# Summing a graph layer's spare blocks by node on VectorE in place of one-hot products on TensorE

## The chip, the cores and the metric

The kernel runs on one core of one Trainium2 chip. The metric is the device time of one execution in microseconds; the time of a kernel is the median of several runs.

## The reference

A graph of 6250 nodes with 256 channels and 100,000 edges (`src`, `dst`, with `dst` sorted) goes through four layers. In each, every node adds to its own row the rows of the sources of its edges, and a small network with three weight matrices follows:

```python
def agg(h):
    return jax.ops.segment_sum(h[src], dst, num_segments=N)
for l in range(NL - 1):                      # layers 0, 1, 2
    h = x + agg(x)
    h = jax.nn.relu(h @ W1s[l] + b1s[l])
    h = jax.nn.relu(h @ W2s[l] + b2s[l])
    x = h @ W3s[l] + b3s[l]
h = x + agg(x)                               # layer 3, the head
h = jax.nn.relu(h @ cW1 + cb1)
h = jax.nn.relu(h @ cW2 + cb2)               # 64 channels
return h @ cW3 + cb3
```

Before the first layer `x` is layer-normalized and rectified; at the end the given `x` is added. All of it is fp32. Since a layer is linear up to its first bias, the kernel keeps rows already multiplied by the next layer's W1, so that a layer starts with the sum over edges and then adds the bias.

## The kernel before

The nodes are cut into 49 blocks of 128. `sorted_edges` sums a block's edges in one of two ways.

- **Multiplied blocks.** The edge counts between all source nodes and the block's 128 nodes form a matrix, which layer 0 builds once (`build`, L1002) from one-hot products: 32 bf16 products `bp` a block (L1024), their one-hots `lo` and `hi` made on VectorE (L983), the sums cast to uint8 by ScalarE or VectorE (L1032, L1034), and the block written to a DRAM matrix (`mats`). Up to four blocks are a panel. `product` (L1450) runs over a panel in 49 units, one for each block of source nodes. A unit is four matmuls `agg` (L1469): the two halves of the 256 channels, and for each the high and the low part of the rows (`XY` holds both for all 49 blocks). The panel's counts are fetched by SyncE (`fetch`, L1043) and cast to fp32 into a ring `a` by ScalarE (L1444) or VectorE (L1446) some units ahead.
- **Gathered blocks.** `Gathered` (L1248) fetches the rows of the edges by indirect DMA on GpSimd, 128 edges a time and 18 times a block (L1293), and adds them up on TensorE with one-hots of 32 columns (`sums`, L1337), which VectorE makes (L1318), in two visits a block. VectorE then adds the block's own row and the sums into `u` (L1354, L1363), TensorE turns it (`pt`, L1371), and ScalarE adds bias and rectifies (L1379).

Both kinds then go through `mlp` (L1128): second product (L1140, or L1154 in the head), third product (L1203, L1184), and the result is stored to the next layer's table in DRAM and split again into high and low part in `XY` (`split`, `reload`).

Layer 0 has 27 multiplied blocks in seven panels and 22 gathered ones; layers 1 to 3 have 31 multiplied blocks in eight panels, the first of three blocks, and 18 gathered ones.

The order is written out by hand: every engine's instructions come in the order in which the program issues them. `product` advances unit by unit; a planner keeps a clock of its own in which every step has a price (`passed`, `work_of`), and spreads the gathers of a layer evenly over its expected length (`Gathered.begin`, `flow`, `send`), each tied by `after` to a TensorE instruction. A layer's gathers begin when the last store of the layer before has been issued. `LEAD` (21 us) is how far rows are asked for ahead of their visit.

Ahead of layer 0 comes the setup: `look` (L604) finds for each half block where its edges begin (`first`), asks for the edges by indirect DMA on GpSimd (`ask`, L598; eight requests are issued at once behind `starts`), and turns them into the one-hot codes `clT` and the gather lists `idx` and `rel`; `normed` (L811) normalizes, multiplies by W1 and stores the first table, interleaved step by step with `look`. If `look` finds the edges unfit (`good` is 0), the general program `any_edges` runs behind.

Of the kernel before, what the change touches and what calls it, by code (L numbers as in the profile page):

```python
# [8 lines left out]
F32 = mybir.dt.float32  # L9
I32 = mybir.dt.int32  # L10
# [386 lines left out]
def sorted_edges(  # L397
# [72 lines left out]
    S0 = 2 * panels[0][0]  # L470
    assert gone[-2] == panels[-1] and sorted(
        b + i for b, n in gone[:-2] + gone[-1:] + panels for i in range(n)) == list(range(NT))
# [13 lines left out]
    clT = const.tile([P, 2, GSUB, NSUB - S0], BF16, name="clT")  # L486
# [7 lines left out]
    tables = [dram.tile([N, C], F32, name=f"table{l}") for l in range(NLAYER + 1)]  # L494
    w31d = [dram.tile([P, (KC + 1) * C], F32, name=f"w31_{l}") for l in range(NLAYER)]
    mats = [dram.tile([P, n, NT * P], U8, name=f"mat{p}") for p, (_, n) in enumerate(panels)]
# [107 lines left out]
    def look(pool):  # L604
# [27 lines left out]
        junk = pool.tile([P, NEAR], BF16, name="junk", bufs=1)  # L632
        for h in range(2):
# [5 lines left out]
                                    op0=OP.is_lt, op1=OP.add, accum_out=half[:NSUB, h:h + 1])  # L639
        at = pool.tile([P, 1], F32, name="at_f", bufs=1)  # L640
# [15 lines left out]
        place = pool.tile([P, 1], F32, name="place", bufs=1)  # L656
        nc.gpsimd.iota(place, pattern=[[0, 1]], base=0, channel_multiplier=P,
# [43 lines left out]
        for q in range(NQ):  # L701
            nc.tensor.matmul(ps[:PW, 2 * q:2 * q + 2], sel[:NSUB, q, :], both[:NSUB, :],
                             start=True, stop=True)
        spread = pool.tile([P, NQ, 2], F32, name="spread", bufs=1)
# [7 lines left out]
        for q, (b, _) in enumerate(gone):  # L712
            nc.vector.tensor_scalar(part[:PW, q:q + 1], part[:PW, q:q + 1], place[:PW, 0:1],
                                    float(T * P * b), op0=OP.add, op1=OP.add)
# [16 lines left out]
        for q0 in range(0, GSUB, H):  # L731
# [180 lines left out]
    with tc.manual_schedule():  # L912
# [38 lines left out]
        def load_weights(l):  # L951
# [15 lines left out]
        batches = [(p, s, q0) for p, (b0, n) in enumerate(panels)  # L967
                   for s in range(2 * b0, 2 * (b0 + n)) for q0 in range(0, GSUB, BATCH)]
# [4 lines left out]
        def pair(hots, k):  # L973

            if k < len(batches):
                s = batches[k][1]
                pairs[s] = hots.tile([P, 2, GSUB, 2], BF16, name="pairs", bufs=3)
                nc.scalar.copy(pairs[s], clT[:, :, :, s - S0, None].to_broadcast([P, 2, GSUB, 2]))
# [23 lines left out]
        def build(hots, ats, ps_b):  # L1002
# [7 lines left out]
            for k, (p, s, q0) in enumerate(batches):  # L1010
                i, half = divmod(s - 2 * panels[p][0], 2)
# [5 lines left out]
                for q in range(0, BATCH, 2):  # L1017
# [17 lines left out]
                    if half and q0 + q + 2 == GSUB:  # L1035
                        own = at[:, panels[p][0] + i, :]
                        nc.vector.tensor_tensor(own, own, ident, OP.add)
                        nc.sync.dma_start(out=mats[p][:, i, :], in_=at.rearrange("p h d -> p (h d)"))
# [4 lines left out]
        def fetch(l, p):  # L1043

            n = panels[p][1]
            c = len(mat.setdefault((l, p), [])) * P
            at = chunks.tile([P, 4, CH * P], U8, name="at", bufs=5)
            nc.sync.dma_start(out=at[:, :n, :], in_=mats[p][:, :, c:c + CH * P])
# [199 lines left out]
        class Gathered:  # L1248
            def __init__(self, l):
# [3 lines left out]
                               for q, (b, n) in enumerate(gone) for i in range(n)  # L1253
                               if l == 0 or (b, n) != panels[-1]]
                self.alone = {b + i for b, n, i, _ in self.blocks}
                self.visits = [(g, rounds) for g in range(len(self.blocks)) for rounds in VISITS[l > 0]]
# [136 lines left out]

        EARLY = 8
        PRE = (GSUB * panels[0][1] + EARLY) // 2
        last = [len(panels) - 1 - (l == 0) for l in range(NLAYER + 1)]
# [3 lines left out]
        LEAD, TAIL = 21.0, 10.0  # L1400
        COLS, FULL32, TURN, VISIT, BUILD, BURST = 0.457e-3, 1.68e-3, 0.4, 1.7, 0.2, 0.3
# [196 lines left out]
```

## Time and profile before

| | |
|---|---|
| median of 3 runs (lowest, highest) | 2200.67 us (2200.57, 2204.43) |
| the profiled execution's own time | 2198.92 us |
| its span, first to last instruction | 2197.0 us |
| mean granted TensorE clock | 0.987 |
| setup, to the first `agg` product | about 161 us |
| layer 0 | about 561 us |
| layers 1, 2 and 3 | about 502, 502 and 471 us |

Lines of the profile read so: the line of the program, the engine, the operation, the tiles (out<-in), shapes, the count, then the busy time in us, the mean ns of one, and the idle time of the engine just before them with what ended it. PE is TensorE's matmul, PEld its weight load, DVE VectorE, ACT ScalarE, POOL GpSimd, SP SyncE. An fp32 matmul shows as two records. A timeline row begins with the start and the duration in us; a row of the waits gives who waited for whom, the total in us, the times and sometimes the longest.

### The profile page before, as it was taken

How to read it: one execution, taken by the hardware profiler on the slowest of the kernel's cores; microseconds unless marked ns; L12 is line 12 of the kernel's file. 1: busy time of each engine (PE TensorE's matmuls, PEld its weight loads, DVE VectorE, ACT ScalarE, POOL GpSimd, SP SyncE). 2: the span in 40 equal slices, each digit the busy share in tenths (PEclk: the TensorE clock that was granted, in tenths of full speed). 3: DMA queues.
4: the chain of work that ended last, by engine and by line, in shares of the span. 5: the costliest groups of instructions: out<-in, count | busy, mean ns of one | idle time of the engine just before them, and what ended most of it. 6: DMA issues, size and time to landing. Idle time of an engine off the chain costs nothing.

```text
span 2197.0 us, 34423 instructions
## 1 busy us (share of the span) xinstructions
PE 2122.9 (97%) x12100; PEld 1558.0 (71%) x12100; DVE 946.2 (43%) x2738; ACT 941.8 (43%) x1919; POOL 1412.0 (64%) x1442
## 2 busy tenths in 40 slices
PE   5869999999999999999999999999999999999997
PEld 3648667666666877777777877777777877777775
DVE  7878556555554532322234423222233433333332
ACT  4768667566665422233224432232223433323331
POOL 3617777777775466666666366666666277777772
PEclk9969999999999999999999999999999999999999
DMA  5535566566565655544555655545555566656653
GB/s 159 164 123 195 188 191 190 174 187 194 166 216 182 198 153 151 161 138 146 154 165 177 190 155 152 161 132 160 151 168 165 162 198 189 183 171 185 198 180 92
DMA packets 251438, 371.52 MB, mean 169 GB/s; under 512 B 32728, under 2 KB 201964, under 8 KB 251254
## 3 DMA queue, kind: packets, MB, share of 16 engines
q0 software_dynamic: 67264, 181.96, 28.4%
q1 hardware_dynamic: 182062, 185.40, 26.7%
q8 instruction: 97, 1.59, 0.3%
q10 hardware_dynamic: 1928, 1.85, 0.3%
q14 instruction: 87, 0.71, 0.1%
HBM read 311.02 MB, written 58.07 MB: 168 GB/s over the span
## 4 chain that ended last, share of the span: by engine, by line
PE 90%; ACT 3%; DVE 3%; DMA 2%; issue 1%; POOL 0%; SPq 0%; ACTq 0%; DVEq 0%
PE agg L1469 62%; PE sums L1337 10%; PE ps L1203 6%; PE ps L1140 6%; PE bp L1024 4%; ACT at L1032 1%; PE pt L1371 1%; DMA back<-table 1%; PE ps L1154 1%; PE ps L1184 1%; ACT a L1444 0%; PE ps L573 0%; DVE zs L879 0%; DVE stats L831 0%; DVE XY L888 0%
## 5 line engine op out<-in xcount | busy, mean ns | idle before, releaser
L1293 POOL DMA_INDIRECT rows<-table,idx x1368 | 1358.5, 993 | 698.4 <-PE agg L1469 363.1
L1469 PE MATMUL agg<-a,XY 128*128 128x512 f32 (+1 forms) x6076 | 1479.1, 396 | 8.1 <-ACT a L1444 5.1
L1469 PEld LDWEIGHTS agg<-a,XY 128*128 128x128 f32 x6076 | 1108.1, 189 | 281.5 <-issue 49.8
L1444 ACT CAST a<-at 128x512 fp32r<-128x512 uint8 (+1 forms) x943 | 559.9, 609 | 627.5 <-PE agg L1469 599.6
L1446 DVE CAST a<-at 128x512 fp32r<-128x512 uint8 (+1 forms) x576 | 271.0, 474 | 547.7 <-PE agg L1469 523.9
L1032 ACT CAST at<-bp 128x392 uint8<-128x392 f32 x386 | 174.9, 491 | 168.7 <-PE bp L1024 167.1
L1337 PE MATMUL sums<-rows,hot 128*32 128x256 f32 x3344 | 230.4, 384 | 1.6 <-DMA rows<-table,idx 1.5
L1337 PEld LDWEIGHTS sums<-rows,hot 128*32 128x32 f32 x3344 | 103.6, 109 | 112.0 <-issue 48.2
L1024 PE MATMUL bp<-hi,lo 128*128 128x196 bf16 x992 | 139.6, 262 | 12.7 <-DVE hi L983 6.4
L983 DVE TENSOR_TENSOR hi<-cols,pairs 128x784 bf16<-128x784 bf16 x248 | 139.0, 561 | 0.0
L983 DVE TENSOR_TENSOR lo<-lanes,pairs 128x512 bf16<-128x512 bf16 x248 | 104.8, 423 | 78.4 <-PE bp L1024 50.3
L1024 PEld LDWEIGHTS <-lo 128*128 128x128 bf16 x992 | 76.8, 100 | 85.3 <-issue 37.0
L1363 DVE TENSOR_TENSOR u<-u,sums 128x256 f32<-128x256 f32 x76 | 31.8, 419 | 239.3 <-PE agg L1469 239.3
L1203 PE MATMUL ps<-w,h 128*128 128x256 f32 x588 | 133.8, 380 | 0.0
L1140 PE MATMUL ps<-h,w 128*128 128x512 f32 (+2 forms) x336 | 133.2, 540 | 0.0
L1318 DVE TENSOR_TENSOR hot<-colf,rel 128x64 f32<-128x64 f32 x836 | 127.6, 220 | 0.0
L1203 PEld LDWEIGHTS ps<-w,h 128*128 128x128 f32 x588 | 110.5, 190 | 14.4
L1034 DVE CAST at<-bp 128x392 uint8<-128x392 f32 x110 | 62.3, 567 | 130.1 <-PE bp L1024 129.9
L1208 DVE TENSOR_TENSOR zz<-ps,w 128x512 f32<-128x512 f32 (+1 forms) x78 | 50.7, 659 | 121.4 <-PE ps L1203 121.4
L1140 PEld LDWEIGHTS ps<-h,w 128*128 128x128 f32 x336 | 60.6, 190 | 52.5 <-issue 44.7
L1143 ACT ACTIVATE h<-ps,bias 128x512 f32<-128x512 f32 (+2 forms) x84 | 52.0, 636 | 92.7 <-PE ps L1140 92.4
L1379 ACT ACTIVATE h<-pt,bias 128x256 f32<-128x256 f32 (+1 forms) x84 | 33.5, 450 | 125.9 <-PE pt L1371 125.8
(136 smaller groups left out, 749.0 us busy)
## 6 DMA issues: line engine op xcount, KB each, us to landing
at<-mat SPq DMA_DIRECT2D x189, 448.0 KB
mat<-at SPq DMA_DIRECT2D x31, 784.0 KB
rows<-table,idx POOLq DMA_INDIRECT x1368
table<-zz SPq DMA_DIRECT2D x69, 256.0 KB
back<-table SPq DMA_DIRECT2D x118, 128.0 KB
at<-mat SPq DMA_DIRECT2D x28, 336.0 KB
xs<-in_x_dram SPq DMA_DIRECT2D x8, 768.0 KB
table<-zs SPq DMA_DIRECT2D x24, 256.0 KB
```

What stands on the lines that cost most here:

```text
L983: nc.vector.tensor_tensor(o.rearrange("p q (n t) -> p q n t", t=2), values.rearrange("p (n t) -> p n t", t=2)[:, None, :, :].to_broadcast( ...
L1024: mm = nc.tensor.matmul(bp[:, m * HW:(m + 1) * HW], lo[:, q + m, :], hi[:, q + m, :], start=True, stop=True)
L1032: nc.scalar.copy(o, v)
L1034: nc.vector.tensor_copy(o, v)
L1140: mm = nc.tensor.matmul(ps[:, :w], weights[l][0][:, c, i * P:(i + 1) * P], h1[:, c, :w], start=(c == 0), stop=(c == KC - 1))
L1203: mm = nc.tensor.matmul(o, h2[0][:, c, nodes], w3[:, c, :], start=(c == 0), stop=(c == KC - 1))
L1293: got = nc.gpsimd.indirect_dma_start(out=t, out_offset=None, in_=tables[self.l][:, :], in_offset=bass.IndirectOffsetOnAxis(ap=idx[:, o:o + ...
L1318: nc.vector.tensor_tensor(hot[:, i, :, :], colf[:, None, i * Q:(i + 1) * Q].to_broadcast([P, 2, Q]), rel[:, o + k:o + k + TS + 1:TS, None] ...
L1337: nc.tensor.matmul(self.sums[(2 * h + m) * Q:(2 * h + m + 1) * Q, :C], self.hots[r, m][:, h, :], self.rows[g, h, k], start=(r == 0), stop= ...
L1444: nc.scalar.copy(o, mat[l, p][j])
L1446: nc.vector.tensor_copy(o, mat[l, p][j])
L1469: mm = nc.tensor.matmul(agg[c][:, :w], XY[:, j, o:o + P], a[:, :w], start=(j == 0 and half == 0), stop=(j == NT - 1 and half == 1))
```

## The change

Layers 1 to 3 now gather blocks 32 to 48 (17 blocks, `NODES`) by node: `ByNode` replaces `Gathered`. For each block, 17 gathers each bring one edge of every node (nodes with fewer edges read a row of zeros, 128 of which stand behind each table), and two more bring up to 256 surplus rows of nodes with over 17 edges. TensorE adds the surplus rows with two one-hot products of full width into one half of the bank of `sums` (`spare`), ScalarE copies the seventeenth row into the other half (`seed`), and VectorE adds the other 16, two at a time, into the bank (`pair`), then both halves into `u`. The lead of the gathers is 12 us (`LAG`), and a layer has 11 buffers of two rows where it had 26 of one.

The other 32 blocks are multiplied, in eight panels of four; layer 0 still multiplies 27 of them, in panels that start with one of three and so straddle the stored matrices, and builds all 32. VectorE casts every fourth unit's counts in layers 1 to 3, where it did every second.

The lists for the new gathers (`idxN`, `relN`) are made by `nodes` during layer 0, one step every second unit: degrees by comparing and a product with ones, running sums, the runs of edges by 17 indirect DMAs from `padded` (a copy of `src` that `look` makes), and for the surplus two picking products for each block. Layer 0 has 18 row buffers, before 24. In `look`, the block starts `begins` come from a new product, whose left side `whole` is copied on GpSimd.

```diff
-    gone = [(0, 4), (4, 4), (8, 4), (12, 4), (16, 1), (44, 4), (48, 1)]
-    panels = [(17, 3), (20, 4), (24, 4), (28, 4), (32, 4), (36, 4), (40, 4), (44, 4)]
+    RANKS, KR, PAD = 17, 44, P
+    NODES = [(32, 4), (36, 4), (40, 4), (44, 4), (48, 1)]
+    gone = [(32, 4), (36, 4), (40, 4), (44, 4), (27, 1), (28, 4), (48, 1)]
+    early = [(0, 3)] + [(b, 4) for b in range(3, 27, 4)]
+    wide = [(b, 4) for b in range(0, 32, 4)]
+    panels = [early] + [wide] * NLAYER
...
         for q in range(NQ):
             nc.tensor.matmul(ps[:PW, 2 * q:2 * q + 2], sel[:NSUB, q, :], both[:NSUB, :],
                              start=True, stop=True)
+        whole = pool.tile([P, P], F32, name="f", bufs=1)
+        nc.gpsimd.tensor_copy(whole[:NSUB], first[:NSUB, 0:1].to_broadcast([NSUB, P]))
+        nc.tensor.matmul(ps[:, 2 * NQ:2 * NQ + NG], whole[:NSUB, :],
+                         ident[:NSUB, 2 * G0:2 * (G0 + NG):2], start=True, stop=True)
+        nc.vector.tensor_copy(begins, ps[:, 2 * NQ:2 * NQ + NG])
         spread = pool.tile([P, NQ, 2], F32, name="spread", bufs=1)
...
-                    nc.scalar.copy(o[:, q0 + i:q0 + i + 4, :],
-                                   ps[:, :4 * NSUB].rearrange("p (q s) -> p q s", q=4)[:, :, S0:])
+                    v = ps[:, :4 * NSUB].rearrange("p (q s) -> p q s", q=4)
+                    nc.scalar.copy(o[:, q0 + i:q0 + i + 4, :], v[:, :, :2 * BUILT])
+                    if t is r:
+                        nc.scalar.copy(cN[:, q0 + i:q0 + i + 4, :], v[:, :, 2 * G0:])
...
+        class ByNode:
...
+                cols = [RANKS, RANKS + 1, RANKS - 1] + list(range(RANKS - 1))
...
+                    self.acts += [(k + 1, self.spare, (g,)), (k + 2, self.seed, (g,))]
+                    self.acts += [(k + 4 + i, self.pair, (g, i)) for i in range(0, RANKS - 1, 2)]
...
+            def spare(self, g):
...
+                for h in range(2):
+                    mm = nc.tensor.matmul(sums[:, :C], hot[:, h, :], rows[:, h, :],
+                                          start=(h == 0), stop=(h == 1))
...
+            def seed(self, g):
+                rows = self.rows.pop((g, RANKS - 1))
+                after(nc.scalar.copy(sums[:, C:], rows[:, (RANKS - 1 - RANKS) % 2, :]),
+                      "one engine at a time in a bank", self.last)
...
+            def pair(self, g, i):
+                rows = self.rows.pop((g, i))
+                nc.vector.tensor_tensor(sums, sums, rows.rearrange("p h c -> p (h c)"), OP.add)
...
+                if i == RANKS - 3:
+                    u = self.u
+                    nc.vector.tensor_tensor(u, u, sums[:, C:], OP.add)
+                    nc.vector.tensor_tensor(u, u, sums[:, :C], OP.add)
+                    self.finish(b, n, q, u)
...
+        def nodes(pool, ps_b):
...
+                ps = ps_b.tile([P, W], F32, name="bp")
+                for g in range(m):
+                    nc.tensor.matmul(ps[:, g:g + 1], own[:, g].rearrange("p h q t -> p (h q t)"),
+                                     one_b, start=True, stop=True)
+                nc.vector.tensor_copy(deg[:, 0, g0:g0 + m], ps[:, :m])
...
+                    ps = ps_b.tile([P, W], F32, name="bp")
+                    for t in range(2):
+                        nc.tensor.matmul(ps[:, t * (R2 + 2):(t + 1) * (R2 + 2)], picks[t],
+                                         ox[:, g, :], start=True, stop=True)
+                    nc.vector.tensor_copy(got[:, g].rearrange("p t r -> p (t r)"),
+                                          ps[:, :2 * (R2 + 2)])
...
-                if l == 0 or j % 2 == 0:
+                if l == 0 or j % 4:
                     nc.scalar.copy(o, mat[l, p][j])
                 else:
                     nc.vector.tensor_copy(o, mat[l, p][j])
...
+                if beside is not None and u >= PRE + 16 and u % 2 == 0:
+                    next(sorted_nodes, None)
```

More of the change, by code (lines that the diff above doesn't have):

```diff
@@ L493, in sorted_edges @@
     eps = const.tile([P, 1], F32, name="eps")
-    tables = [dram.tile([N, C], F32, name=f"table{l}") for l in range(NLAYER + 1)]
+    tables = [dram.tile([N + (PAD if l else 0), C], F32, name=f"table{l}")
+              for l in range(NLAYER + 1)]
+    padded = dram.tile([E + KR], I32, name="padded")
     w31d = [dram.tile([P, (KC + 1) * C], F32, name=f"w31_{l}") for l in range(NLAYER)]
-    mats = [dram.tile([P, n, NT * P], U8, name=f"mat{p}") for p, (_, n) in enumerate(panels)]
+    mats = [dram.tile([P, n, NT * P], U8, name=f"mat{p}") for p, (_, n) in enumerate(wide)]
     def rows_io(ap, t0, n, sb, load):
@@ L1009, in build @@
             step = 0
-            for k, (p, s, q0) in enumerate(batches):
-                i, half = divmod(s - 2 * panels[p][0], 2)
+            for k, (b, s, q0) in enumerate(batches):
+                half = s % 2
                 if half == 0 and q0 == 0:
@@ L1394, in sorted_edges @@
         EARLY = 8
-        PRE = (GSUB * panels[0][1] + EARLY) // 2
-        last = [len(panels) - 1 - (l == 0) for l in range(NLAYER + 1)]
+        PRE = (GSUB * FIRST + EARLY) // 2
+        last = [len(panels[l]) - 1 for l in range(NLAYER + 1)]
         units = [(0, -1, j) for j in range(PRE)] + [
```

308 lines of the change are left out of this document (273 added, 35 removed).

## The prediction

> **What bounds the kernel now.** I read part 1 of the page, then the busy time by stage, then single stages. The rows by stage cover the setup (0 to 161 us), layer 0 and layers 1, 2 and 3; after the length come the busy times of PE, PEld, DVE, ACT and POOL.
>
> ```profile
> PE 2122.9 (97%) x12100; PEld 1558.0 (71%) x12100; DVE 946.2 (43%) x2738; ACT 941.8 (43%) x1919; POOL 1412.0 (64%) x1442
> 0.00:161.00 161.00, 109.17 (x522) 78.25 (x522) 127.16 (x330) 96.99 (x217) 62.52 (x82) 0.88 0.48 147
> 161.00:722.00 561.00, 553.39 (x3548) 389.10 (x3548) 325.29 (x912) 368.58 (x818) 403.34 (x388) 1.00 0.59 186
> 722.00:1224.00 502.00, 502.00 (x2705) 375.32 (x2704) 163.36 (x499) 165.26 (x310) 314.14 (x324) 1.00 0.54 161
> 1224.00:1726.00 502.00, 502.00 (x2702) 375.25 (x2701) 162.97 (x498) 165.00 (x307) 315.13 (x324) 1.00 0.54 159
> 1726.00:2197.00 471.00, 456.33 (x2630) 340.07 (x2628) 167.45 (x503) 145.96 (x270) 316.90 (x324) 0.99 0.58 175
> ```
>
> Layers 1 to 3 are TensorE from end to end, with VectorE at a third. Layer 0 is TensorE with 7.6 us of gaps. Only the setup has another bound: VectorE, 127 of 161 us. So in layers 1 and 2 what leaves PE is time gained. Layer 3 needs a second look, at the gathers:
>
> ```profile
> L1293 POOL DMA_INDIRECT rows<-table,idx x324: 947/953/1747, 738.5 to 1206.0; - x162
> L1293 POOL DMA_INDIRECT rows<-table,idx x324: 947/953/1782, 1742.1 to 2157.6; - x162
> POOL rows L1293 <- issue: 52.1, 171, 0.3
> POOL rows L1293 <- PE agg L1469: 41.9, 136, 0.5
> 2170.34 0.38 PE L1371 MATMUL pt<-ident,u 128*128 128x128 f32 x2
> 50.38 3.37 DMA ws<-in_src_dram,starts
> ```
>
> The first two rows (layers 1 and 3: durations min/median/max, first and last start) give a gather every 1.447 us in layer 1 and every 1.286 us in layer 3. Layer 3's waits are about 0.3 us each: POOL is back to back there, 0.98 us a gather and 0.3 between. That stream can't be hurried, and the change keeps its length (17 x 19 = 323 gathers for 18 x 18 = 324).
>
> **Layers 1 and 2.** The matmul groups of layer 2, and the stretches that give a pitch:
>
> ```profile
> L1337 PE MATMUL sums<-rows,hot 128*32 128x256 f32 x792 | 54.1, 384 | 0.0
> L1203 PE MATMUL ps<-w,h 128*128 128x256 f32 x196 | 44.6, 380 | 0.0
> L1371 PE MATMUL pt<-ident,u 128*128 128x128 f32 x36 | 6.8, 272 | 0.0
> 1737.97 19.77 PE L1469 MATMUL agg<-a,XY 128*128 128x384 f32 x112
> 2109.37 11.51 PE L1469 MATMUL agg<-a,XY 128*128 128x512 f32 x48
> ```
>
> Removed per layer: the 18 blocks' one-hot products, 54.1 us. Added: two full products per block, in shape those of L1203 (128x128 weights, 256 columns, two records each), so 4 x 44.6/196 = 0.91 us, 15.5 us for 17 blocks. The three-block panel becomes four blocks wide: 196 matmuls go from 19.77/112 = 0.1765 to 11.51/48 = 0.240 us, +12.4. One turn fewer: -0.4. Sum -26.6. I give back 2.5 us for the switches of weights around the new products (0.15 each, between 0 and 0.3) and 1 us for waits at the bank of `sums`: **-23 us a layer, -46 for two**, between -27 and -15.
>
> Does VectorE hide its new work?
>
> ```profile
> L1208 DVE TENSOR_TENSOR zz<-ps,w 128x512 f32<-128x512 f32 x69 | 47.0, 690 | 115.9 <-PE ps L1203 115.9
> L1318 DVE TENSOR_TENSOR hot<-colf,rel 128x64 f32<-128x64 f32 x836 | 127.6, 220 | 0.0
> L1363 DVE TENSOR_TENSOR u<-u,sums 128x256 f32<-128x256 f32 x76 | 31.8, 419 | 239.3 <-PE agg L1469 239.3
> L1446 DVE CAST a<-at 128x512 fp32r<-128x512 uint8 x504 | 233.6, 463 | 544.4 <-PE agg L1469 520.5 <-ACT a L1444 15.2 <-issue 6.2
> L1444 ACT CAST a<-at 128x512 fp32r<-128x512 uint8 x819 | 499.6, 624 | 613.9 <-PE agg L1469 594.8 <-issue 11.3 <-ACT XY L1099 3.5
> ```
>
> No row writes a sum back into PSUM; the nearest is L1208, PSUM plus SBUF at 512 columns, 0.69 us, and I take it for each pair add. Per layer 136 adds are 94 us, the second add into `u` 7, the new one-hots about 7; 198 small one-hots (44) and 88 casts (41) go. VectorE rises from 163 to about 186 of 479 us, ScalarE by 88 x 0.624 plus the seeds to about 227. Both are covered. In the order of the changed program the last pair add of a block stands two or three units of 49 in a panel (1.9 to 2.9 us) ahead of the next block's product in 46 of 51 cases, and has 0.69 + 2 x 0.42 = 1.5 us behind it. The casts' 520 us of waiting for PE say that VectorE has run ahead until its buffers were full, so those 1.5 us end in time; without that lead each block would pay up to 1 us.
>
> The gathers fit too: layer 1 starts them some 17 us in, 322 x 1.27 = 409 us, landing 3.4 (50.38 row): 430, where the last add stands at about 462.
>
> **Layer 3.** The first gather came 16.1 us after the layer's start; in the changed order the last store before it stands three units earlier, so 13.3. Then the stream, the landing, 1.5 us of adds, and 26.7 us from the last turn (2170.34) to the end of the span. What is a gather's pitch?
>
> ```profile
> 950.51 0.90 DVE L1318 TENSOR_TENSOR hot<-colf,rel 128x64 f32<-128x64 f32 x6
> 951.33 1.25 POOL L1293 DMA_INDIRECT rows<-table,idx  x1 [0.41 <-PE agg L1469]
> 916.95 0.69 DVE L1208 TENSOR_TENSOR zz<-ps,w 128x512 f32<-128x512 f32 x1 [1.04 <-PE ps L1203]
> 916.32 0.95 POOL L1293 DMA_INDIRECT rows<-table,idx  x1 [0.39 <-PE ps L1203]
> ```
>
> The slow gather lies against small one-hots, whose two inputs are in SBUF; the one beside an add from PSUM keeps 0.95. Most of the former go and adds of the latter kind come: I take 0.965 + 0.305 = 1.27 us. 13.3 + 408.9 + 3.4 + 1.5 + 26.7 = 453.8 against 471: **-17**, where PE alone would give -23. At the old 1.286 it is -12, at 0.953 it is -21. [...]
>
> **Setup.**
>
> ```profile
> 41.43 1.00 POOL L598 DMA_INDIRECT wd<-in_dst_dram,starts  x1 [4.32 <-DVE both L696]
> 50.38 0.97 POOL L598 DMA_INDIRECT ws<-in_src_dram,starts  x1 [0.30 <-issue]
> 43.52 0.17 DVE L705 COPY spread<-ps 72x14 f32<-72x14 f32 x1 [1.23 <-PE ps L702]
> 60.00:80.00 20.00, 17.89 (x95) 14.28 (x95) 18.95 (x53) 16.11 (x35) 15.43 (x16) 1.00 0.70 196
> 100.00:127.00 27.00, 18.80 (x92) 14.63 (x91) 19.84 (x53) 15.18 (x36) 1.75 (x3) 0.94 0.26 85
> 23.66 3.78 PE L573 MATMUL ps<-w1n,w3t 128*128 128x256 f32 x8 [1.22 <-ACT w3t L564]
> 38.76 2.00 PE L573 MATMUL ps<-w1n,w3t 128*128 128x256 f32 x8 [1.28 <-ACT w3t L564]
> ```
>
> The copy to `whole` is put on POOL behind the eight edge requests (first and eighth row). They end at 51.35, the copy at about 51.9; the new product waits for it on PE, with layer 0's transposes and products queued behind, and `begins` waits on VectorE ahead of `spread` and all of the normalizing. VectorE goes on at about 52.7, not 43.5: 9.2 us, on the engine that is 95% busy (18.95 of 20). Added copies for `cN` make it **+9.5**. The 7 us that VectorE idles from 100 to 127 could take back as much (+2.5). On the other side, the same eight products of L573 took 3.78 us soon after the idle beginning and 2.00 later: if TensorE is slow again after this wait, once or twice 1.8 us more (+13). [...]
>
> **Layer 0.** It keeps 22 gathered blocks and 27 multiplied ones, and builds 32 blocks for 31.
>
> ```profile
> 664.03 0.51 PE L1024 MATMUL bp<-hi,lo 128*128 128x196 bf16 x4
> 664.32 1.18 PE L1469 MATMUL agg<-a,XY 128*128 128x512 f32 x4
> L1203 PEld LDWEIGHTS ps<-w,h 128*128 128x128 f32 x588 | 110.5, 190 | 14.4
> L702 PE MATMUL ps<-both,near_i 98*72 98x2 f32 x14 | 1.0, 204 | 0.5 <-ACT w L575 0.5
> PEld L1024 <- DVE lo L983: 11.0, 40, 0.4
> ```
>
> The added block: eight times four matmuls at 0.29 us (664.03 to 664.32) and 0.08 for the switch, 3 us. Sorting by node (`nodes`): 17 pairs of fp32 products with 128 columns of weights and 29 moving columns. They are bound by their four loads: 0.19 each by L1203, so 0.76 plus 0.2 for the switch, 16 us; the L702 records (72 columns, 1.0/14) would make it 9. The degree counts, nine times 0.3, add 3. About 306 small VectorE operations at the 0.22 us of L1318's 64 columns make 65 us; VectorE goes from 325 to about 400 of 590 us. 28 of them wait for a product just issued, with the one-hots (0.42 and 0.56 us) behind them that PE needs next; PEld's 11 us for them today is what is exposed where VectorE has more room. I add 6 us, between 0 and 28. **+28**, between 12 and 55.
>
> Costed at nothing: the copy of `src` into `padded` on ACT's queue (0.8 MB of traffic in a setup whose DMA engines are half busy, row 0 to 161) and six zero stores on SP; the panels' fetches, two transfers for one on SP where a panel straddles two matrices; 17 edge gathers on POOL, which with its 388 gathers at 1.04 + 0.3 us would be busy 544 of 589 us; and 18 row buffers for 24, still two visits' rows (10 + 8). These last two hide under the gathers' lead; if that is gone, PE waits for rows in layer 0, which I would put at up to 10 us and count into the bounds.
>
> **Sum.** 9.5 + 28 - 46 - 17 = -25.5. The profiled execution took 2198.92 us (span 2197.0), so 2173.4; the median of the runs shown is 1.75 higher: **2175 us**.
>
> **The rivals.**
>
> *Quicker (chance 0.18).* Gathers run at the 0.953 floor, so layer 3 gives -21, and the sort's loads go at the L702 rate with no exposed waits, layer 0 +15: sum -42.5, 2158. For it: 0.953 is the median already.
>
> *The sort holds VectorE (0.12).* Each of the 28 waits exposes one set of one-hots, 1 us: layer 0 +50, 2197. For it: VectorE at two thirds there. Against: the PE queue is never short of `agg` for long.
>
> *Waits at the bank (0.08).* VectorE is not ahead, 34 blocks of layers 1 and 2 pay 0.8 us (layer 3 has room under its gathers): +27, 2202. Against it: the casts' 520 us.
>
> *The adds hold the gathers, slower (0.10).* Were the pair adds like the small one-hots, each costs a gather the 0.3 us seen at 951.33: 136 x 0.3 = 41 us of stream per layer. All of it shows in layer 3, and in layers 1 and 2 the 9 us beyond their 32 of slack: +59, 2234. It decides from 0.19 us an add on, where it eats the 25.5. Against: the 916 rows.
>
> *The fast path is not taken (0.02).* A node with over 44 edges, or a block with over 256 surplus rows, clears `good` and the general program runs behind, far over 2300. Counting the fixed inputs gives at most 32 edges and 191 surplus rows.
>
> **How the numbers follow.** The forecast has 0.50, with its own range 2157 to 2192. A measurement of this kernel tells about 0.2% from no change, 4.4 us either way. Faster: 0.50 x 0.96, the quicker rival, half of the sort's and a third of the bank's: 0.75. Slower: the held gathers, the general program, a fifth of the sort's and 0.3 of the bank's: 0.17. Same: 0.08. The range 2150 to 2206 takes in the costs' bounds and the middle rivals and leaves out 2234.
>
> **What would show it.** Right: `spread` near 52.7 us; layer 0 near 590 us long; layers 1 and 2 near 479 us at full PE; in layer 3 gathers from end to end, 1.27 us apart, and PE waiting near its end; pair adds near 0.69 us. Wrong: PE waiting for `sums` in layers 1 and 2, gathers over 1.05 us beside the adds, or gaps before the `bp` products in layer 0.

## The result, and the profile after

The kernel after takes **2152.46 us** (median of 4 runs, 2150.22 to 2154.61), the kernel before beside it 2200.62 (2199.99 to 2204.43): a ratio of 0.978, 95% interval 0.976 to 0.979, 48 us less. Forecast were 2175 us, 25.5 less. On three other chips the kernel before takes 6 to 8% longer; after ran unchanged on one of them, where it takes 11% longer and the gain is not there. That has a part of its own under the experiments.

Both profiles can be cut at the same places: at the first product of layer 0, and where VectorE takes the last panel of a layer out of PSUM. The row that marks this is the same in both kernels (start, duration, line); first before, then after:

```profile
718.07 0.75 DVE L1482 TENSOR_SCALAR h<-agg,bias 128x512 f32<-128x512 f32 x1 [6.68 <-PE agg L1469]
1223.09 0.75 DVE L1482 TENSOR_SCALAR h<-agg,bias 128x512 f32<-128x512 f32 x1 [2.52 <-PE agg L1469]
1725.54 0.75 DVE L1482 TENSOR_SCALAR h<-agg,bias 128x512 f32<-128x512 f32 x1 [2.52 <-PE agg L1469]
```

```profile
166.36 1.65 PE L1773 MATMUL agg<-a,XY 128*128 128x384 f32 x4 [3.26 <-ACT a L1746]
750.15 0.75 DVE L1786 TENSOR_SCALAR h<-agg,bias 128x512 f32<-128x512 f32 x1 [6.67 <-PE agg L1773]
1222.76 0.75 DVE L1786 TENSOR_SCALAR h<-agg,bias 128x512 f32<-128x512 f32 x1 [2.24 <-PE agg L1773]
1692.46 0.75 DVE L1786 TENSOR_SCALAR h<-agg,bias 128x512 f32<-128x512 f32 x1 [5.06 <-PE agg L1773]
```

The first product of the kernel before starts at 161.45 us; the spans are 2197.0 and 2149.2.

| stage | before | after | change | forecast |
|---|---|---|---|---|
| setup, to the first product of layer 0 | 161.45 | 166.36 | +4.9 | +9.5 |
| layer 0 | 556.6 | 583.8 | +27.2 | +28 |
| layer 1 | 505.0 | 472.6 | -32.4 | -23 |
| layer 2 | 502.5 | 469.7 | -32.8 | -23 |
| layer 3 and the end | 471.5 | 456.7 | -14.7 | -17 |
| span | 2197.0 | 2149.2 | -47.8 | -25.5 |

Busy time by stage after (length; then PE, PEld, DVE, ACT, POOL; granted clock, DMA share, GB/s):

```profile
0.00:166.00 166.00, 107.32 (x524) 76.95 (x524) 126.95 (x331) 97.49 (x221) 64.32 (x84) 0.86 0.47 145
166.00:750.00 584.00, 568.00 (x3657) 398.97 (x3657) 387.08 (x1245) 373.55 (x827) 423.90 (x405) 0.99 0.58 182
750.00:1223.00 473.00, 470.14 (x1981) 367.51 (x1981) 192.70 (x382) 218.23 (x412) 311.62 (x323) 1.00 0.57 172
1223.00:1692.00 469.00, 469.00 (x1972) 366.25 (x1971) 187.88 (x377) 215.25 (x409) 312.49 (x323) 1.00 0.57 172
1692.00:2149.00 457.00, 431.65 (x1894) 331.88 (x1892) 199.65 (x387) 201.60 (x375) 315.96 (x323) 0.97 0.60 182
```

Layers 1 and 2 are still TensorE from end to end: VectorE took on the adds (188 to 193 us of a layer, 186 forecast) and TensorE waits for it nowhere in these two layers. Layer 3 no longer is: TensorE is busy 432 of 457 us. Its waits there (us, times, longest), and the new operations as groups over the span (count, busy time, mean ns):

```profile
PE pt L1536 <- DVE u L1527: 7.3, 5, 3.5
PE sums L1496 <- DMA rows<-table,idxN: 4.0, 2, 3.6
```

```profile
L1464 POOL DMA_INDIRECT rows<-table,idxN x969 | 940.1, 970 | 448.1 <-PE agg L1773 172.2
L1510 DVE TENSOR_TENSOR sums<-sums,rows 128x512 f32<-128x512 f32 x408 | 283.4, 695 | 410.3 <-DMA rows<-table,idxN 207.4
```

A pair add takes 0.695 us (0.69 taken). In the setup PE waits for the copy to `whole` as forecast: the product of L725 starts behind it at 52.15 us, and `spread` is ready to follow at 52.88 (52.7 forecast, 43.52 before).

```profile
52.15 0.61 PE L725 MATMUL ps<-ident,f 98*128 98x17 f32 x2 [8.24 <-POOL f L724]
52.88 0.16 DVE L729 COPY spread<-ps 72x14 f32<-72x14 f32 x1
```

### The profile page after: what moved, and what is told of

Its sections match the earlier page's. It is cut to its first block, busy times and chain, and to the rows that moved or that the text cites. A ratio compares the mean times of both kernels' runs of the same rounds, so it can differ in the third digit from the quotient of the medians.

```text
span 2149.2 us, 30951 instructions
## 1 busy us (share of the span) xinstructions
PE 2046.1 (95%) x10025; PEld 1541.6 (72%) x10025; DVE 1094.3 (51%) x2721; ACT 1106.1 (51%) x2240; POOL 1428.3 (66%) x1458
## 4 chain that ended last, share of the span: by engine, by line
PE 86%; DVE 6%; DMA 4%; ACT 2%; issue 2%; POOL 1%; SPq 0%; ACTq 0%; DVEq 0%; POOLq 0%
PE agg L1773 62%; PE ps L1234 6%; PE ps L1171 6%; PE bp L1049 4%; PE sums L1367 3%; PE sums L1496 2%; DMA rows<-table,idxN 2%; ACT at L1057 1%; DVE ws L691 1%; PE ps L1215 1%; PE pt L1536 1%; DVE hi L1008 1%; DVE zs L905 0%; PE ps L1185 0%; DVE lo L1008 0%
## 5 line engine op out<-in xcount | busy, mean ns | idle before, releaser
L1773 PE MATMUL agg<-a,XY 128*128 128x512 f32 (+1 forms) x6076 | 1520.9, 402 | 9.9 <-ACT a L1746 6.1
L1773 PEld LDWEIGHTS agg<-a,XY 128*128 128x128 f32 x6076 | 1121.5, 189 | 277.9 <-issue 20.7
L1464 POOL DMA_INDIRECT rows<-table,idxN x969 | 940.1, 970 | 448.1 <-PE agg L1773 172.2
L1746 ACT CAST a<-at 128x512 fp32r<-128x512 uint8 (+1 forms) x1207 | 706.6, 617 | 258.9 <-PE agg L1773 240.0
L1323 POOL DMA_INDIRECT rows<-table,idx x396 | 414.2, 1046 | 187.2 <-issue 62.0
L1510 DVE TENSOR_TENSOR sums<-sums,rows 128x512 f32<-128x512 f32 x408 | 283.4, 695 | 410.3 <-DMA rows<-table,idxN 207.4
L1748 DVE CAST a<-at 128x512 fp32r<-128x512 uint8 x312 | 137.0, 440 | 225.9 <-PE agg L1773 191.7
L1504 ACT COPY sums<-rows 128x256 f32<-128x256 f32 x51 | 19.2, 377 | 213.1 <-PE sums L1496 204.2
L1171 PEld LDWEIGHTS ps<-h,w 128*128 128x128 f32 x320 | 58.1, 189 | 54.1 <-issue 45.5
L1131 DVE TENSOR_TENSOR XY<-back,XY 128x256 fp32r<-128x256 f32 x120 | 50.2, 423 | 80.0 <-ACT XY L1130 79.4
L1367 PE MATMUL sums<-rows,hot 128*32 128x256 f32 x968 | 70.0, 385 | 5.1 <-DMA rows<-table,idx 5.0
```

Of the source, the lines that this page charges most:

```text
L1171: mm = nc.tensor.matmul(ps[:, :w], weights[l][0][:, c, i * P:(i + 1) * P], h1[:, c, :w], start=(c == 0), stop=(c == KC - 1))
L1323: got = nc.gpsimd.indirect_dma_start(out=t, out_offset=None, in_=tables[self.l][:, :], in_offset=bass.IndirectOffsetOnAxis(ap=idx[:, o:o + ...
L1367: nc.tensor.matmul(self.sums[(2 * h + m) * Q:(2 * h + m + 1) * Q, :C], self.hots[r, m][:, h, :], self.rows[g, h, k], start=(r == 0), stop= ...
L1464: got = nc.gpsimd.indirect_dma_start(out=t[:, h, :], out_offset=None, in_=tables[self.l][:, :], in_offset=bass.IndirectOffsetOnAxis(ap=idx ...
L1510: nc.vector.tensor_tensor(sums, sums, rows.rearrange("p h c -> p (h c)"), OP.add)
L1746: nc.scalar.copy(o, mat[l, p][j])
```

## The experiments

The first four ran once each on a chip where the kernel before takes 2197.6 us; they are read layer by layer, from the marker rows, against the profiles above. Layer 0, whose code the first three leave as it was, took 557.1 us there for 556.6, and 584.0 and 586.2 for 583.8, so a difference below some 3 us tells nothing.

**What a one-hot product cost (before).**

```diff
-                for r in rounds:
+                times = (1, 0, 2, 1)[self.l]
+                for r, s in [(r, s) for r in rounds for s in range(times)]:
```

> The kernel before, with layer 1's one-hot products left out (its sums are stale) and every one of layer 2's issued twice in a row; layers 0 and 3 as they were. Layers 1 and 2 took 505.0 and 502.4 us. Theory 1 (a visit costs PE its products and the change of weights and stream on either side, 1.43 + 0.24 us, so the term of 54.1 us that the prediction took off was too small): layer 1 falls by 60 us to about 445; layer 2, where the second products bring no further change of stream, rises by 36 x 1.43 = 51 us to about 554. Theory 2 (the 54.1 us of busy time is all there was, and the rest of the gain came from elsewhere): layer 1 falls by 54 us to 451, layer 2 rises by 54 us.

The marker rows at the ends of its layers 0 to 2, from the timeline:

```profile
719.68 0.75 DVE L1483 TENSOR_SCALAR h<-agg,bias 128x512 f32<-128x512 f32 x1 [6.68 <-PE agg L1470]
1165.68 0.75 DVE L1483 TENSOR_SCALAR h<-agg,bias 128x512 f32<-128x512 f32 x1 [2.52 <-PE agg L1470]
1714.56 0.75 DVE L1483 TENSOR_SCALAR h<-agg,bias 128x512 f32<-128x512 f32 x1 [2.52 <-PE agg L1470]
```

Layer 1 without them takes 446.0 us, 59.0 less, with PE still busy in 444.2 of them; layer 2 with them twice takes 548.9, 46.4 more. So a visit costs 59.0 / 36 = 1.64 us on PE, and its products issued once more 46.4 / 36 = 1.29. The 0.35 between the two I read as the change from one stream to the other and back; no run measures it by itself. Theory 1 holds: the term to take off was 59, not 54. Both theories put the doubling too high (51 and 54): the busy time of this group (1.50 us a visit) is not the price of its products, it is more than what they cost issued once more (1.29) and less than what goes when they go (1.64).

**What a surplus product costs (after).**

```diff
-                for h in range(2):
-                    mm = nc.tensor.matmul(...)
+                for _ in range((0, 0, 2, 0)[self.l]):
+                    for h in range(2):
+                        mm = nc.tensor.matmul(...)
```

> The kernel after, with the two products per block that take the surplus rows left out in layers 1 and 3 (those rows are not added) and issued twice in layer 2. Layers 1 to 3 took 472.6, 469.7 and 456.7 us with the tail. Theory 1 (two products of 0.43 us and the changes of stream around them, about 0.2 us a block, are all that a block costs PE): layer 1 falls by 17 x 1.08 = 18 us, layer 2 rises by 17 x 0.87 = 15 us, layer 3 stays within 3 us because its gathers set the time. Rival for layers 1 and 2 (PE also stands at the bank of sums behind VectorE's adds, hidden in the busy time): layer 1 falls by 22 us or more. Rival for layer 3 (PE sets the time): it falls by 15 us or more.

Its marker rows, layers 0 to 2:

```profile
752.34 0.75 DVE L1788 TENSOR_SCALAR h<-agg,bias 128x512 f32<-128x512 f32 x1 [6.68 <-PE agg L1775]
1211.91 0.75 DVE L1788 TENSOR_SCALAR h<-agg,bias 128x512 f32<-128x512 f32 x1 [2.24 <-PE agg L1775]
1696.34 0.75 DVE L1788 TENSOR_SCALAR h<-agg,bias 128x512 f32<-128x512 f32 x1 [5.06 <-PE agg L1775]
```

Layer 1 without them takes 459.6 us, 13.0 less; layer 2 with them twice 484.4, 14.7 more; layer 3 without them, to its end at 2148.6, 452.3, 4.5 less. So a block's two products cost 0.77 to 0.87 us, and leaving them out saves no more than issuing them again costs: there is no change of stream on top (0.2 was expected; that part of theory 1 fell). Nothing is hidden at the bank of `sums`: that would have shown as 22 us or more. Layer 3 gives back 4.5, a little over the 3 expected and far from 15.

**Who sets which layer (after).**

```diff
+                self.top = RANKS - 1 if l == 2 else RANKS - 3
-                cols = [...] + list(range(RANKS - 1))
+                cols = [...] + list(range(self.top))
...
-                nc.vector.tensor_tensor(sums, sums, rows..., OP.add)
+                for _ in range(2 if self.l == 2 else 1):
+                    nc.vector.tensor_tensor(sums, sums, rows..., OP.add)
```

> The kernel after, with two of the 19 gathers of a block and the pair add that takes them left out in layers 1 and 3 (two ranks are not added), and every pair add of layer 2 issued twice (its sums are wrong). Theory 1 (layers 1 and 2 are set by PE, layer 3 by the gathers): layer 1 stays within 2 us of 472.6; layer 2, with 94 us more of adds on VectorE, within 3 us of 469.7, its gathers still near 0.97 us each; layer 3 loses 34 x 1.28 = 43.5 us of its stream, of which it can give back what PE waited for rows and sums there, 11 us, and up to 20 with the end of the kernel nearer to PE. Rival 1 (the adds hold the gathers, or VectorE has no room): layer 2 grows by 10 us or more and its gathers pass 1.05 us. Rival 2 (layer 3 is set by PE and the end of the kernel): layer 3 stays within 3 us.

Marker rows of this kernel; then the gathers of layer 2 as a group, in it (L1465) and in after (L1464); then its busy time in layers 2 and 3:

```profile
754.65 0.75 DVE L1788 TENSOR_SCALAR h<-agg,bias 128x512 f32<-128x512 f32 x1 [6.67 <-PE agg L1775]
1229.65 0.75 DVE L1788 TENSOR_SCALAR h<-agg,bias 128x512 f32<-128x512 f32 x1 [5.06 <-PE agg L1775]
1698.27 0.75 DVE L1788 TENSOR_SCALAR h<-agg,bias 128x512 f32<-128x512 f32 x1 [5.06 <-PE agg L1775]
```

```profile
L1465 POOL DMA_INDIRECT rows<-table,idxN x323 | 312.1, 966 | 159.4 <-PE agg L1775 87.1 <-issue 35.1 <-PE ps L1171 8.6
```

```profile
L1464 POOL DMA_INDIRECT rows<-table,idxN x323 | 312.5, 967 | 156.9 <-PE agg L1773 49.6 <-issue 38.7 <-DMA back<-table 38.2
```

```profile
1230.00:1697.00 467.00, 467.00 (x1966) 365.20 (x1964) 281.99 (x517) 216.54 (x410) 312.05 (x323) 1.00 0.58 174
1697.00:2120.00 423.00, 422.11 (x1890) 327.97 (x1888) 186.75 (x367) 201.84 (x375) 280.23 (x289) 1.00 0.61 185
```

- Layer 1 with 34 gathers less takes 475.0 us, 2.4 more, and nothing is won: its gathers do not set it. The 2.4 is no more than its layer 0 was longer too (586.2 for 583.8, by the same instructions).
- Layer 2 with all pair adds doubled takes 468.6, 1.1 less than after, with VectorE at 282 us instead of 188 and the gathers at 966 ns instead of 967. VectorE has the room, and 136 adds more left the mean gather as it was: the adds do not hold the gathers, and both rivals of the prediction that rested on this are out.
- Layer 3 with 34 gathers less takes 429.6 us to the end of the span at 2127.9, 27.1 less, and TensorE is full there (422 of 423). So in after the gathers hold back 27 us of layer 3, more than PE's waits of 11 us and the 20 us that I allowed: PE is idle in 25.5 us of it in all, and only 14.6 of these are waits between its instructions; the rest lies behind its last one.

**What the sort's products cost.**

```diff
-                    for t in range(2):
+                    for t in [0, 1] * 3:
                         nc.tensor.matmul(ps[...], picks[t], ...)
```

> The kernel after, with the products of the sort by node (two per block of 128 weights columns and 29 moving ones, 68 records in the profile) issued three times over into the same place, 136 records more in layer 0, which took 583.8 us. By the prediction's price for them (16 us for the 17 pairs, bound by their loads and a change of stream): +32 us. By their busy time in the profile after (9.1 us for 68): +18 us, theory 1. Rival (they stand in gaps of PE that the one-hots of the build leave anyway): under 8 us.

The timeline at both ends of its layer 0, and the group of the products:

```profile
168.89 1.65 PE L1773 MATMUL agg<-a,XY 128*128 128x384 f32 x4 [3.32 <-ACT a L1746]
769.67 0.75 DVE L1786 TENSOR_SCALAR h<-agg,bias 128x512 f32<-128x512 f32 x1 [6.68 <-PE agg L1773]
```

```profile
L1666 PE MATMUL bp<-ox,pick 128*128 128x29 f32 x204 | 24.3, 267 | 0.0
```

Layer 0 takes 600.8 us, 17.0 more for 136 records: 0.125 us each, so the 68 of the change cost 8.5, not 16 (7.3 if layer 0 is taken as the 586.2 us of the run before). The price is near that of their busy time, theory 1; neither the prediction's 32 us nor the rival's 8 came.

**Three edits for the two places where after lost.** These and the later runs were made on other chips, and there every kernel took longer: beside the first four of them the kernel before took 2368.8 us (17 runs), beside the next two 2343.1 (9) and beside the last two 2347.6 (11), for 2200.6. What follows compares only kernels that ran on the same chip.

```diff
-        nc.gpsimd.tensor_copy(whole[:NSUB], ...)
+        nc.vector.tensor_copy(whole[:NSUB], ...)
```

> The kernel after, with the copy to `whole` made by VectorE, which has its source, and no longer by POOL behind the eight edge requests. In the profile after PE stood 8.2 us and VectorE 10.1 us for it, at 52 us. Theory 1 (that wait is the setup's whole loss, and about half of it was made good by idle time of VectorE later in the setup): the first product of layer 0 starts 5 us earlier, near 161.5 us, and the kernel takes 5 us less than after, near 2147. The prediction's own sum: 9 us less, 2143. Rival (the setup ends with the edges that POOL asks for, and the wait is hidden): within 1 us of 2152.

```diff
-                if beside is not None and u >= PRE + 16 and u % 2 == 0:
-                    next(sorted_nodes, None)
                 prepare(...)
                 if beside is not None:
                     ... next(beside) ...
+                if beside is not None and u >= PRE + 16 and u % 2 == 0:
+                    next(sorted_nodes, None)
```

> The kernel after, with each step of the sort by node written out behind the build's steps of the same unit of layer 0, not ahead of them; the same instructions. PE's matmuls of the build stood 8.9 us idle in layer 0, of it 4.9 behind VectorE's one-hots, against 1.5 us before. Theory 1 (a step of the sort that stands ahead of a one-hot, and waits for a product of its own, holds the one-hot and with it PE): most of 5 us goes, the kernel takes 4 us less than after, near 2148. Rival (the next unit's one-hots wait as long): within 1 us of 2152.

```diff
-    name="rings", bufs=AHEAD + 2) ... name="gath", bufs=18
+    name="rings", bufs=AHEAD + 1) ... name="gath", bufs=20
-    prepare(u + 1 + (AHEAD if l == 0 else AHEAD + 2))
+    prepare(u + 1 + (AHEAD - 1 if l == 0 else AHEAD + 2))
```

> The kernel after, with 20 row buffers in layer 0 for 18, and the room taken from the buffers of cast adjacency columns (4 for 5, casts one unit later). PE waited 5.0 us for rows late in layer 0 (1.5 us before, with 24 buffers). Theory 1 (18 buffers hold the gathers back): the wait falls to 2 or 3 us, the kernel takes 2 to 3 us less, if the casts still come in time. Rival (the gathers of the end of the layer are as late as the queue makes them): the wait stays at 5; or the lost cast buffer costs 3 us and more in waits of the products for casts.

> The kernel after, unchanged, beside the other three on the same chip: 2152 us, between 2149 and 2155 by the runs so far; its distance to the others is what they are read from.

| kernel | median us | runs | to before, 95% | first product | layer 0 |
|---|---|---|---|---|---|
| after again | 2387.4 | 6 | 1.0067 (1.0045 to 1.0088) | 169.7 | 663.4 |
| `whole` on VectorE | 2392.4 | 6 | 1.0092 (1.0067 to 1.0116) | 174.5 | 661.3 |
| sort behind the build | 2397.9 | 5 | 1.0115 (1.0093 to 1.0136) | 170.7 | 673.9 |
| 20 row buffers | 2377.6 | 12 | 1.0038 (1.0025 to 1.0052) | 170.7 | 650.8 |

None of the three theories came out as told.

- *`whole`.* PE's wait of 8.2 us at L725 is gone (that product starts at 43.40 us, for 51.81 beside it), but the first product of layer 0 starts at 174.5 us, 4.8 later than beside it. Three later profiles with this edit start it at 170.7, 172.6 and 171.5 us, the three here without it at 169.7 to 170.7: on none of these chips did the setup get shorter when the wait went, so there the wait was hidden. What the edit brings on a chip like the first stays open.
- *The order.* The sort's own products then wait where the one-hots had waited: PE's wait ahead of the sort's products for ScalarE's evictions of the build grew from 6.1 us (five times) to 14.7 (nine times, the row below, from the waits of layer 0), and layer 0 is 10.5 us longer. Both kinds of products share the two `bp` buffers; theory 1 fell.

```profile
PE bp L1666 <- ACT at L1057: 14.7, 9, 5.3
```

- *The rows.* 9.8 us less than after, layer 0 12.6 less. The sign that the theory named did not come: PE's wait for rows is 3.2 us with 20 buffers and 3.1 with 18 on this chip. But the gathers of layer 0 run from 171.0 to 812.5 us with 18 buffers and from 172.0 to 800.8 with 20, 12.7 us shorter. That fits the theory's cause (18 buffers hold the gathers back); since the buffers of casts changed too, it is not shown.

Two kernels with more than one of the edits, on another chip:

> The kernel after, with the copy to `whole` on VectorE and each step of the sort by node written behind the build's steps of its unit: both of those edits in one kernel, read stage by stage against the undisturbed profile of after (first product of layer 0 at 166.4 us, layer 0 583.8 us long from there). Theory for the copy: the 8.2 us that PE waits at 52 us go, and the first product of layer 0 starts 3 to 5 us earlier. Rival: the setup ends with the edges that POOL asks for, and the first product starts within 1 us of 166.4. Theory for the order: PE's 4.9 us of waits for the build's one-hots fall to 1 or 2 and layer 0 is 3 us shorter. Rival: within 1 us. In all 2145 us by both theories, 2152 by both rivals.

> The kernel of the run before this, and 20 row buffers in layer 0 for 18, with one buffer of cast adjacency columns less. Theory: the 5.0 us that PE waits for rows in layer 0 fall to 2 or 3, layer 0 is 2 to 3 us shorter than without it, 2142 us. Rival 1: the rows are as late as the gathers' queue makes them, the wait stays near 5 and the time is that of the run without it. Rival 2: with a buffer less the products wait for casts, 3 us longer or more.

2378.7 us for the two edits (1.0146, 1.0130 to 1.0162) and 2365.9 with the row buffers too (1.0096, 1.0081 to 1.0112): the row buffers bring 12.8 us here as well (layer 0 668.9 and 650.2 us), PE's wait for rows is again the same (3.4 and 3.6), and neither beats before. The time of 2142 to 2152 that the theories named was not to be had on such a chip, so the edits are not tested for the first one.

**Why the gain is not there on those chips.**

> The kernel before, unchanged, for a profile beside those of the runs in which it took 2343 to 2369 us and the kernel after 2387. If it is as slow again, its four layers (556.6, 505.0, 502.4 and 471.5 us in the first profile) tell where it loses less than after, which lost 79.6 us in layer 0, 47.3 and 40.8 in layers 1 and 2 and 64.8 in layer 3 with the tail. Theory 1 (stalls without a cause in the profile strike each engine alike, and cost time where a chain of engines is tight: the sort by node in layer 0, the adds in the bank of sums, the gathers of layer 3): before loses under 60 us in layer 0 and under 55 in layer 3, and as much as after, 40 to 47 us, in layers 1 and 2. Theory 2 (the stalls are PE's alone, so many for each of its instructions): before, with 12100 matmuls for 10000, loses a fifth more than after in each layer. If it is undisturbed, 2198 us, with no such waits.

> The kernel with the three edits (copy to `whole` on VectorE, the sort's steps behind the build's, 20 row buffers) once more, for its stages. Where before takes 2198 us: first product of layer 0 at 162 to 163 us (theory; rival 166), PE's waits for the build's one-hots in layer 0 1 to 2 us (rival 5), its waits for rows 2 to 3 us (rival 5), 2142 us in all (rival 2152). Where before takes 2343 us or more: about 2366 us again, a ratio near 1.010, and layer 0 shorter than the 663 us of after by 10 us or more.

The three edits again came to a ratio of 1.0081 (1.0053 to 1.0109), first product at 171.5 us, layer 0 at 651.8. The profile of before there, by stage, and then that of after from the other set:

```profile
168.00:785.00 617.00, 569.57 (x3536) 394.69 (x3536) 321.56 (x904) 364.82 (x811) 399.26 (x388) 0.98 0.54 169
785.00:1300.00 515.00, 508.69 (x2703) 374.51 (x2704) 157.38 (x504) 163.55 (x313) 321.61 (x324) 1.00 0.53 157
1300.00:1811.00 511.00, 506.04 (x2706) 374.16 (x2705) 154.37 (x498) 162.18 (x308) 320.24 (x324) 1.00 0.53 157
1811.00:2343.00 532.00, 487.82 (x2637) 347.46 (x2635) 163.68 (x503) 144.26 (x271) 322.64 (x324) 0.97 0.52 155
```

```profile
170.00:833.00 663.00, 594.93 (x3657) 410.27 (x3657) 388.22 (x1245) 374.38 (x826) 421.63 (x405) 0.97 0.52 160
833.00:1353.00 520.00, 487.02 (x1980) 373.14 (x1980) 192.60 (x381) 214.27 (x411) 315.16 (x323) 0.98 0.52 156
1353.00:1863.00 510.00, 485.20 (x1974) 369.55 (x1973) 187.91 (x377) 213.20 (x409) 314.71 (x323) 0.98 0.53 158
1863.00:2385.00 522.00, 459.41 (x1895) 341.01 (x1893) 199.65 (x387) 197.74 (x375) 315.34 (x323) 0.95 0.54 160
```

Neither theory fits. Before loses 60 us in layer 0, 11 and 9 in layers 1 and 2, and 60 in layer 3; after loses 80, 47, 41 and 65. But the lengths themselves agree: layers 1 and 2 take 510 to 520 us with either kernel, though they need 502 to 505 and 470 to 473 of TensorE on the first chip. And the streams of gathers agree. These are the gathers of layers 1, 2 and 3 (shortest, median and longest in ns, then first and last start), of before and of after:

```profile
L1293 POOL DMA_INDIRECT rows<-table,idx x324: 951/957/1760, 805.6 to 1285.6; - x162
L1293 POOL DMA_INDIRECT rows<-table,idx x324: 951/957/1800, 1317.3 to 1793.8; - x162
L1293 POOL DMA_INDIRECT rows<-table,idx x324: 951/957/1776, 1828.2 to 2306.0; - x162
L1464 POOL DMA_INDIRECT rows<-table,idxN x323: 950/957/1284, 859.2 to 1334.5; - x162
L1464 POOL DMA_INDIRECT rows<-table,idxN x323: 951/957/1207, 1369.4 to 1846.3; - x162
L1464 POOL DMA_INDIRECT rows<-table,idxN x323: 950/957/1483, 1877.1 to 2352.2; - x162
```

A stream takes 475 to 480 us in each of them, 1.475 to 1.486 us a gather, though the median gather itself takes 957 ns, for 953 and 957 on the first chip. There the streams of before took 467, 467 and 416 us and those of after 425, 430 and 413. So they are 13, 9 and 62 us longer in before and 50, 47 and 62 in after, each within 6 us of what its layer lost. That is what a slower stream of gathers would give that sets layers 1 to 3 with both kernels: the change keeps its length (323 gathers for 324), and work taken off TensorE is then worth nothing. It is not shown to be the cause: each gather is tied to a TensorE instruction, so a TensorE that is held up would draw the stream out too, and no run on these chips changed the number of gathers.

The transfers themselves took no longer. These are the rows of the gathers' queue (packets, MB, share of 16 engines' time) in the two profiles of before, first chip first:

```profile
q0 software_dynamic: 67264, 181.96, 28.4%
q0 software_dynamic: 67264, 181.96, 26.6%
```

28.4% of 2197.0 us and 26.6% of 2343.6 are 624 and 623 us. The lower rates there (155 to 160 GB/s from layer 1 on, for 159 to 175 in before and 172 to 182 in after on the first chip) are the same bytes in a longer time.

What holds the gathers, or TensorE, stays open. It is not the granted clock alone: before lost 11 and 9 us in layers 1 and 2 with a granted clock of 1.00. The longest of PE's waits there, by the waits of before, is one for nothing that the profile names,

```profile
PE agg L1469 <- issue: 23.6, 59, 1.0
```

and PE's wait for rows grew only from 1.5 to 3.2 us. But that trace holds only a third of the records of semaphores raised by transfers (9,881 for 31,364 in the first one of before), so a wait without a name may be one whose end was not recorded. No run here shows what these waits are.

## Why the prediction was right, point by point

- **Direction and range.** Faster was given 0.75, and 2152 lies in the range (2150 to 2206), at its low end: the likeliest case's mechanism came true and one term was too small. It is nearer to the *quicker* rival (2158), but not for its reasons: gathers did not run at its 0.953 us in layer 3 (315.96 us for 323, 0.978 in the mean), and layer 0 cost 27, not 15.
- **The mis-sized term: layers 1 and 2, -46 forecast, -65.2 measured.** Per layer the products removed were put at 54.1 and are worth 59.0; the products added at 15.5 + 2.5 + 1, and are worth 13.0 to 14.7. I read the removed visits' price from the busy time of their group (54.1 / 36 = 1.50 us a visit, measured 1.64), and charged changes of weights to the products added, where none shows: the 0.15 us for each was my estimate, no run shows it, and leaving the products out saves 13.0 us where issuing them again costs 14.7. The wider panel I took at 0.240 - 0.1765 us a matmul, from two stretches whose lengths include the end of their last matmul. Two stretches of each kind, from the same timelines, give the pitch without it: 52 matmuls of four blocks take 12.48 us and 104 take 24.61, so 0.233 each, and 112 of three blocks take 19.77 and 124 take 21.85, so 0.173; that is 11.8 us for 196, not 12.4. With the measured prices -59.0 + 13.0 to 14.7 + 11.8 - 0.4 = -34.6 to -32.9, against -32.4 and -32.8: what is left over is within what these runs can tell.
- **VectorE covers its new work: right.** 188 to 193 us a layer for 186, no wait of PE for the bank in layers 1 and 2, and twice the adds cost layer 2 nothing. The *waits at the bank* and *the adds hold the gathers* rivals are both shown wrong.
- **Layer 3: -17 forecast, -14.7 measured, by the mechanism named.** First gather 13.6 us after the marker (13.3 forecast), 322 steps of 1.283 us (1.27), 30.0 from the last start to the end (31.6). That the gathers hold it is shown by the run with fewer of them. It also shows that TensorE alone would have needed no more than 429.6 us, 42 less than before, where I had put -23: the gathers hold back more of this layer than I thought.

```profile
L1464 POOL DMA_INDIRECT rows<-table,idxN x323: 950/957/1453, 1706.1 to 2119.2; - x162
```

- **Setup: +9.5 forecast, +4.9 measured.** The 8.2 us wait came where it was put. Behind it the products of the normalizing (rows below, before and after, with the first and last start) start 9.5 us later and end 5.3 us later, so about half was made good between. The prediction had named that (up to 7 us of VectorE's idle time) and did not take it. TensorE's granted clock, 1.00 from 42 to 62 us before, was 0.66 from 42 to 52 and 0.83 from 52 to 62 after, and the first eight records of these products took 2.52 us behind the wait and the next eight 1.89, where the first eights of before took 1.99 and 1.89: the slower TensorE that the prediction feared came for a few us; its price is somewhere in the 4.9. That the wait is the cause of the 4.9 is not shown: in the last two runs, on one chip, the kernel with the three edits (`whole` on VectorE among them) starts these products at 45.3 us, 0.5 later than before (44.8), and still ends them 4.0 later (132.6 for 128.6) and starts layer 0 3.5 later.

```profile
L872 PE MATMUL bp<-w,ht x196: 378/380/632, 44.9 to 122.2; 128*128 128x256 f32 x196
L898 PE MATMUL bp<-w,ht x196: 379/379/797, 54.4 to 127.5; 128*128 128x256 f32 x196
```

- **Layer 0: +28 forecast, +27.2 measured, but the agreement is luck: the parts cancel.** The sort's products cost 7.3 to 8.5 (16 taken, from loads of 0.19 us and 0.2 for a switch; no run shows that the loads bind them, or the switch: a record more cost 0.125), the counts about 2 (3 taken). The products of the build (rows below, layer 0 before and after) are busy 7.0 us more: the added block's 32 at the 115.6 / 880 = 0.131 us of before are 4.2 (3 taken, since I read four matmuls as 0.29 us from one place in the timeline), and the other 2.8 is spread over all of them. PE's idle time there rose from 5.3 to 15.7 us where I had allowed 6: 4.9 for the build's one-hots, the gaps that the prediction gave as a sign of being wrong, and 5.0 for rows are the largest, the latter a cost that I had put at nothing with a bound of 10.

```profile
L1024 PE MATMUL bp<-hi,lo 128*128 128x196 bf16 x880 | 115.6, 251 | 1.5 <-ACT at L1032 0.9
L1049 PE MATMUL bp<-hi,lo 128*128 128x196 bf16 x912 | 122.6, 251 | 8.9 <-DVE hi L1008 4.9 <-DVE at L1059 0.3 <-ACT at L1057 0.3
```

## What to carry to other kernels

- What goes when a stream of small matmuls goes can be more than their busy time, here 1.64 us a visit for 1.50; price a removal by leaving the work out once, and an addition by issuing it twice, before you trust a group's busy time.
- VectorE accumulated in PSUM here (0.695 us for 128x512) beside a gathering GpSimd without holding it: 966 ns a gather with the adds of a layer issued twice, 967 with them once; once the matrix engine was relieved here, the stream of gathers was the next bound in layer 3, and its length in gathers is what counted (27.1 us less with 34 gathers less).
- The gain from relieving one engine was there on one chip (0.978) and not on another (1.0067); run both kernels on more than one chip, and look at the pace of the next bound there, before you call it one.

## What the runs showed of the hardware that I had not expected

- The same two kernels rank differently on different chips: 0.978 on one, 1.0067 on another, where they take 8 and 11% longer. In the two profiles from slower chips, layers 1 and 2 end up equally long with 502 or 470 us of TensorE work in them, and gathers come every 1.475 to 1.486 us in layers 1 to 3 of both kernels, where they come every 1.283 us in layer 3 of after on the first.
- Doubling the products of a visit costs less (1.29 us) than their busy time (1.50), removing them more (1.64).
